# Attention of the first halves: weights from query-by-key scores, turned through VectorE and DRAM

## The chip, the core and the metric

The kernel runs on one core of a Trainium2 chip. The core has a matrix engine (TensorE, PE in the profile; its weight loads are listed as PEld), VectorE (DVE), ScalarE (ACT), GpSimd (POOL) and SyncE (SP), which here only issues transfers. Each engine runs its own queue of instructions in the order in which they were written; an instruction whose inputs are not there yet stops everything behind it on that engine. Data lie in SBUF (128 partitions), matrix results in PSUM, and DRAM is reached by DMA.

The metric is the device time of one execution in microseconds, as the median of several. For the kernel before it is 3506.4 us, from three runs between 3506.35 and 3508.18.

## The reference

One transformer block with modulation by a condition, in float32: 8 sequences of 1024 rows of 512, 16 heads of 32 columns, an MLP of 2048.

```
mod = silu(condition) @ Wada + bada          # shifts, scales and gates, per sequence
xm  = layernorm(x, g1, be1) * (1 + sc_a) + sh_a
q, k, v = split(xm @ Wqkv)                   # 16 heads
scores  = q @ k.T * 32 ** -0.5, causal mask
x = x + gt_a * ((softmax(scores) @ v) @ Wproj + bproj)
xm = layernorm(x, g2, be2) * (1 + sc_m) + sh_m
x = x + gt_m * (gelu(xm @ W1 + b1) @ W2 + b2)
```

The part in question is the softmax and the product with v. In a matrix product on TensorE the summed index lies on the partitions. Scores with queries on the partitions (query by key) give maxima and sums along a row easily, but the product with v needs the weights with keys on the partitions.

## The kernel before

**Blocks.** The 16 half sequences of 512 rows are blocks n = 0 to 15. An even block is the first half of its sequence and attends to its own 512 keys; an odd block attends to its own keys and those of the block before. Heads go in four groups g of four; the four heads of a group sit on 32 partitions each, and their matmuls run side by side.

**Attention.** Because the mask is causal, the 512 x 512 triangle of a group is cut into tiles of 128 rows and 512, 384, 256 or 128 columns, which are packed into *units* of 512 columns by four heads: the widest alone, 384 with 128, and 256 with the 256 of the next group. That makes 2.5 units a group and 10 a block; an odd block has 16 whole units more. Each unit is computed twice:

- A *score unit* (`scores_at_once`, L1588) computes query-by-key scores into the PSUM tile `st`/`sc` (L1595), adds the mask (L1607) and takes row maxima (L1610) on VectorE. `split_maxima` splits the maxima into three bfloat16 parts, and `maxima_rows` turns them into a row per group with small matmuls (L1648).
- A *weight unit* (`weights_T`, L1663) computes the scores once more, now key by query: it starts each PSUM tile with minus the maxima (L1674) and adds the products (L1686). ScalarE takes the exponential (L1698) into a buffer `pT`, POOL zeroes the masked corner (L1703). `weigh` (L1715) multiplies with v (L1726), `add_weights` (L1801) adds the units of a group on POOL (L1816), and `finish` (L1736) sums over keys with a matmul against ones (L1747), inverts on VectorE (L1765) and multiplies on POOL (L1790).

There is a single score tile of four PSUM banks, used by both kinds of units in turn, and three buffers `pT` (`free_p`), handed out when written and given back when read.

**The linear work.** All other products are written as a sequence of steps per window w (`plan`): projections k, q and v, the output projection `proj`, the MLP (`u`, `d`) and the LayerNorm tiles (`at`, `mt`). The large products use Strassen's scheme with seven products of half size; nearly all of them are `matmul` (L217). `at` and `mt` turn normalized rows: VectorE transposes squares of 32 x 32 (L700), the tile is written to DRAM (`held`, L709) and read back with rows and squares exchanged (L714). Weights come through a ring of eight buffers of 256 KB (`fetch`): a load is issued when PE has used the buffer eight pieces before.

**What sets the order.** The program is laid out by a planner at build time. Every helper notes an assumed duration on its engine (`note`, `note_pe`, `note_act`, `note_dma`) and when its result will be there (`written`) or its buffer free (`left`). Linear steps are generators that yield what they wait for. `attend` goes through the blocks; before each unit, `step_aside` lets linear work go ahead until the unit's inputs are due by these assumed times, and a rate (`stream`) spreads the linear work of a window over its units. `until` runs linear work until a condition holds. So each engine's order is fixed before the kernel runs, by assumed times; on the chip an instruction that is reached early simply waits. All weight loads, LayerNorm tiles and results share SyncE's one queue, in the same fixed order.

Of the kernel before, what the change touches and what calls it, by code (L numbers as in the profile page):

```python
# [22 lines left out]
def kernel(  # L23
# [33 lines left out]
    nc = tc.nc  # L57
# [196 lines left out]
    for w in range(1, NB):  # L254
# [182 lines left out]

    cond_act = tmp.tile([P, TB], F32, tag="top", name="cond_act", bufs=1)[:B, :]
    nc.scalar.activation(cond_act, cond_sb, AF.Silu)
# [113 lines left out]
    def add_job(job, reads, first=False):  # L553

        at = sum(1 for other in jobs if other[2]) if first else len(jobs)
        jobs.insert(at, (job, reads, first))

    def run_jobs(everything=False):
        while jobs and (
            everything or (now["DVE"] <= now["PE"] and due(jobs[0][1]) <= now["PE"])  # L560
        ):
            jobs.pop(0)[0]()
# [33 lines left out]
    def hurry():  # L596

        while jobs and due(jobs[0][1]) <= now["PE"] + 500:
# [881 lines left out]
    TRIANGLE = [[0], [1, 3], [2]]  # L1480
    groups = [(n, g) for n in range(NB) for g in range(NC)]

# [175 lines left out]

    free_p = list(range(3))
    first_end, unadded = (0, NC - 1), []  # L1660
    outs, totals = {}, {}

    def weights_T(n, g, parts):  # L1663
# [18 lines left out]
        for k, c0, w, gg in parts:  # L1682
# [11 lines left out]
            note_pe(2.5 * COLUMN * w, "rows", reads, ["st"])  # L1694
        slot = free_p.pop(0)
        pT = pp.tile([P, HPG, TB], F32, tag=f"p{slot}", name=f"pT_{n}_{g}_{parts[0][0]}")
# [39 lines left out]
    def finish(n, g):  # L1736
# [7 lines left out]
        for i, (c0, w, term, held) in enumerate(terms):  # L1744
# [6 lines left out]
            note_pe(2 * COLUMN * w, "columns", [("acc", n, g), ("p", held)], [("l", bank)])  # L1751
        free_p.extend([slot, *(held for *_, held in more)])
# [23 lines left out]
        if (n, g) == first_end:  # L1776
# [5 lines left out]
            return  # L1782

        def quotient():
            invert(3)
            if n == NB - 1 and g == NC - 2:
# [32 lines left out]
    def attend():  # L1819
        previous = None  # L1820
        for n in range(NB):
            h = blocks[n][1]
            slots = []
            mine = sum(exp_need(parts) for g in range(NC) for parts in weight_units(n, g))
            for g in range(NC):
# [4 lines left out]
                for k in range(n_slots):  # L1830
                    upto = len(units)
                    if nxt < len(groups):
# [4 lines left out]
                        if k == n_slots - 1 and nxt + 1 < len(groups):  # L1837
# [36 lines left out]
    def close(n, g, parts, pT, slot, last):  # L1874

        until(lambda: n - blocks[n][1] + parts[-1][0] // NTT in valued)
        own, other = [[part for part in parts if (part[3] == g) == of] for of in (True, False)]
        weigh(n, g, own, pT, slot, last)
        if other:
            shared[n, g + 1] = other, pT, slot  # L1880
        elif parts[0][0] > 0 and (n, g) != first_end:
            free_p.append(slot)
        if parts[0][0] == 0:
            totals[n, g] = (pT, slot)
            if (n, g) in shared:
# [3 lines left out]
                if (n, g) != first_end:  # L1889
                    free_p.append(slot)  # L1890
        if last:
            finish(n, g)

    def next_scores():
# [15 lines left out]

    needs = sum(exp_need(parts) for n in range(NB) for g in range(NC) for parts in weight_units(n, g))
    needs += sum(score_need(*unit) for unit in units)
    for n in range(NB):
# [80 lines left out]
```

## Time and profile before

| what | value |
|---|---|
| median of three runs | 3506.4 us (3506.35 to 3508.18) |
| the profiled execution | 3510.74 us, with a span of 3509.0 us from the first to the last instruction |
| granted TensorE clock | 0.998 |
| busy share of the span | PE 98%, PEld 49%, DVE 63%, ACT 35%, POOL 59% |
| DMA | 491 MB, queue on SyncE 47.1% of 16 engines' span |

The page of the profile has the busy time of each engine, the chain of work that ended last (followed back from the last instruction to what released it), the costliest groups of instructions with the mean of one and the idle time ahead of them, and the DMA queues. The trace gives more: what waited for what, the instructions in order of time, and tables by stretch. A line number names the line of the kernel that issued an instruction. Records of matmuls overlap, so that the cost on PE is better read from start to start. Matmuls in float32 have two records each.

### The profile page before, as it was taken

The numbers are of one execution on the slowest core, as the hardware profiler recorded it, in microseconds if no ns is written. First come the engines' busy times: TensorE is split into PE (matmuls) and PEld (weight loads), VectorE is DVE, ScalarE is ACT, GpSimd is POOL, SyncE is SP. The second block draws the span as 40 slices with busy tenths as digits, with TensorE's granted clock in tenths as the row PEclk, the third lists the DMA queues.
The fourth block names the chain that finished last, engine by engine and source line by source line (L and its number), as shares of the span: only waits on it lengthen the run. The fifth ranks groups of instructions, "written<-read, shape, count | busy, mean of one in ns | idle before, by whom it ended". The sixth has DMA issues, their size and how long they took to land.

```text
span 3509.0 us, 120365 instructions
## 1 busy us (share of the span) xinstructions
PE 3454.3 (98%) x54429; PEld 1724.0 (49%) x54429; DVE 2198.9 (63%) x2401; ACT 1212.4 (35%) x1276; POOL 2084.2 (59%) x2258
## 2 busy tenths in 40 slices
PE   8999999999999999999999999999999999999999
PEld 4444445445554545445454454544555444554445
DVE  5766676564666656665666566765666756656563
ACT  2335333342233423335223342333423343232531
POOL 3767846666366663756727576275753658537660
PEclk9999999999999999999999999999999999999999
DMA  6843444535545445363454534545354544443334
GB/s 212 263 137 104 137 115 140 142 107 159 142 125 156 119 147 153 119 170 115 137 157 130 155 117 144 150 137 148 116 155 137 165 122 146 128 136 101 96 121 140
DMA packets 328194, 491.10 MB, mean 140 GB/s; under 512 B 27260, under 2 KB 177596, under 8 KB 324100
## 3 DMA queue, kind: packets, MB, share of 16 engines
q1 hardware_dynamic: 327568, 483.39, 47.1%
q8 instruction: 428, 7.01, 0.8%
q14 instruction: 82, 0.67, 0.1%
q10 hardware_dynamic: 116, 0.03, 0.0%
HBM read 425.57 MB, written 55.64 MB: 137 GB/s over the span
## 4 chain that ended last, share of the span: by engine, by line
PE 83%; POOL 7%; DMA 3%; DVE 3%; ACT 1%; issue 1%; SPq 1%; ACTq 0%; DVEq 0%; POOLq 0%
PE bank L217 59%; PE sc L1595 8%; PE st L1686 6%; PE po L1726 6%; POOL pT L1816 4%; PE st L1674 2%; PE bank L1747 2%; DMA hat_m<-held_m 1%; DVE mx L1610 1%; POOL hT L170 1%; ACT pT L1698 1%; DMA held_m<-xm_m 1%; PE bank L1648 0%; POOL xr L170 0%; DMA w<-in_L_cond_Wqkv_dram 0%
## 5 line engine op out<-in xcount | busy, mean ns | idle before, releaser
L1816 POOL TENSOR_TENSOR pT<-pT,pT 128x256 f32<-128x256 f32 (+3 forms) x1254 | 1219.7, 1007 | 298.5 <-PE po L1726 181.6
L1698 ACT ACTIVATE pT<-st 128x2048 f32<-128x2048 f32 x288 | 540.9, 1878 | 1065.1 <-PE st L1686 959.8
L217 PE MATMUL bank<-w,hT 128*32 128x256 f32 x14336 | 823.7, 380 | 0.4 <-issue 0.4
L1610 DVE TENSOR_REDUCE mx<-sc 128x4 f32<-128x2048 f32 (+3 forms) x384 | 665.9, 1755 | 235.6 <-PE sc L1595 229.5
L217 PEld LDWEIGHTS bank<-w,hT 128*32 128x32 f32 x14336 | 446.7, 110 | 390.3 <-issue 105.8
L217 PE MATMUL bank<-xm_m,w 128*32 128x256 f32 x8192 | 498.6, 381 | 3.6 <-ACT xm_m L774 2.2
L217 PE MATMUL bank<-t_m,w 128*32 128x256 f32 x6144 | 382.4, 380 | 0.9 <-DVE t_m L786 0.6
L217 PEld LDWEIGHTS bank<-xm_m,w 128*32 128x32 f32 x8192 | 255.6, 110 | 231.2 <-issue 62.2
L1703 POOL TENSOR_SCALAR_AFFINE_SELECT pT<-pT 128x512 f32<-128x512 f32 x256 | 167.5, 672 | 331.9 <-ACT pT L1698 329.4
L1607 DVE TENSOR_TENSOR sc<-sc,mask 128x1024 f32<-128x1024 f32 (+1 forms) x160 | 162.8, 1018 | 293.3 <-PE sc L1595 237.8
L1595 PE MATMUL sc<-kT,qT 32*128 32x512 f32 (+3 forms) x3072 | 329.5, 521 | 4.3 <-ACT pT L1698 3.3
L1726 PE MATMUL po<-pT,v 128*32 128x512 f32 (+3 forms) x3048 | 301.6, 490 | 3.9 <-POOL pT L1703 3.9
L1686 PE MATMUL st<-qT,kT 32*128 32x512 f32 (+3 forms) x3072 | 300.8, 487 | 0.0
L217 PEld LDWEIGHTS bank<-t_m,w 128*32 128x32 f32 x6144 | 189.6, 110 | 172.9 <-issue 48.5
L1765 DVE RECIPROCAL rec<-rec 128x128 f32<-128x128 f32 x256 | 227.3, 922 | 48.2 <-ACT rec L1756 48.2
L217 PE MATMUL bank<-xm_a,w 128*32 128x256 f32 x3968 | 243.4, 382 | 0.4 <-DMA w<-in_L_cond_Wqkv_dram 0.4
L217 PE MATMUL bank<-w,qT 128*32 128x512 f32 x2048 | 237.0, 595 | 1.1 <-DMA w<-in_L_cond_Wproj_dram 0.7
L1595 PEld LDWEIGHTS sc<-kT,qT 32*128 32x128 f32 x3072 | 129.6, 183 | 188.2 <-issue 88.4
L208 DVE TENSOR_TENSOR hT<-bank,u_u 128x512 f32<-128x512 f32 x187 | 126.6, 686 | 105.8 <-PE bank L217 103.1
L217 PE MATMUL bank<-t_a,w 128*32 128x256 f32 x2944 | 183.2, 380 | 0.0
L217 PEld LDWEIGHTS bank<-xm_a,w 128*32 128x32 f32 x3968 | 123.5, 110 | 110.3 <-issue 29.3
L1115 ACT ACTIVATE hT<-hT,cols 128x512 f32<-128x512 f32 x256 | 164.7, 712 | 35.9 <-DVE hT L208 28.5
(243 smaller groups left out, 3404.0 us busy)
## 6 DMA issues: line engine op xcount, KB each, us to landing
w<-in_L_cond_W_dram SPq DMA_DIRECT2D x384, 256.0 KB
w<-kept_up_S SPq DMA_DIRECT2D x256, 256.0 KB
w<-kept_down_S SPq DMA_DIRECT2D x256, 256.0 KB
w<-kept_qkv_S SPq DMA_DIRECT2D x180, 256.0 KB
w<-in_L_cond_Wqkv_dram SPq DMA_DIRECT2D x147, 256.0 KB
hat_a<-in_x_dram SPq DMA_DIRECT2D x64, 256.0 KB
xr<-in_x_dram SPq DMA_DIRECT2D x32, 512.0 KB
w<-in_L_cond_Wproj_dram SPq DMA_DIRECT2D x64, 256.0 KB
```

The lines of the kernel that those rows point to most:

```text
L208: nc.vector.tensor_tensor(out, src, other, op)
L217: nc.tensor.matmul(ps[r, :], columns, rhs, start=start, stop=stop, skip_group_check=True)
L1115: nc.scalar.activation(hT[:, i, :], hT[:, i, :], AF.Gelu, bias=cols[:, O_B1 + f : O_B1 + f + 1])
L1595: nc.tensor.matmul(sc[:, j, c0 : c0 + w], qTs[n][r, gg, ts(qt, P)], keys_of(n, kh)[r, gg, :w], start=True, stop=True, skip_group_check=True,)
L1607: nc.vector.tensor_tensor(place, place, shape_of.to_broadcast(place.shape), ALU.add)
L1610: nc.vector.tensor_reduce(maxima[n, gg][:, kh, qt, :], sc[:, :, c0 : c0 + w], axis=AX.X, op=ALU.max)
L1686: nc.tensor.matmul(st[:, j, c0 : c0 + w], kT[r, gg, ts(k % NTT, P)], qT[r, gg, TB - w :], start=False, stop=True, skip_group_check=True,)
L1698: nc.scalar.activation(pT[:, :, :used], st[:, :, :used], AF.Exp, scale=scale)
L1703: nc.gpsimd.affine_select(diagonal, diagonal, pattern=[[0, HPG], [1, P]], compare_op=ALU.is_ge, fill=0.0, base=0, channel_multiplier=-1,)
L1726: nc.tensor.matmul(po[r, TB - w :], v[:, k % NTT, g * P + j * hd : g * P + (j + 1) * hd], pT[:, j, c0 : c0 + w], start=(k == 0), stop=last ...
L1765: nc.vector.reciprocal(some, some)
L1816: nc.gpsimd.tensor_tensor(into, into, pT[:, j, c0 : c0 + w], ALU.add)
```

## The change

Blocks 2, 4, ..., 14 (all even blocks but the first) compute each unit once. `attend_rows` goes through a block's ten units with `rows_unit`, and `gather` finishes a group:

1. The scores are computed query by key into the score tile, masked, and reduced to row maxima on VectorE as before; the maxima times minus the scale become a bias.
2. ScalarE takes the exponential at once, one head and one tile at a time, with the bias and with the row sums as a second output. It writes into one of the three buffers, with the columns put in an order that suits step 4.
3. VectorE inverts the sums; POOL or ScalarE, whichever the planner sees free earlier, multiplies the weights by them.
4. VectorE transposes the buffer of 128 x 2048 in squares of 32 x 32, in place.
5. Four or eight DMAs, of 32 partitions each, write the squares to a tile in DRAM (`image`) at their place. The buffer is then given back.
6. When all of a group is there, `gather` reads it back as three *pages* with keys on the partitions: two of 1 MB into buffers of the same three, one of 0.5 MB into the tile that `finish` uses for its copies (`top` and `rec` are now two halves of it). Each page is multiplied with v as it lands, in pieces of 256 and 128 columns, and the finished sum is copied into place. There is nothing left to divide.

For these blocks the second score pass, the minus maxima, the split and the rows of maxima, the corner masks, the additions on POOL, the sums over ones and the division fall away. Only one unit at a time may be between step 2 and step 5. The scores of the odd block after a rows block start beside its last units. The odd block's products with v wait until all groups before it are gathered. Blocks 0, 1 and all odd blocks compute as before. In windows of even blocks from 4 on, the projection of v moves behind the output projection and the LayerNorm tile of the block before; the rate of all windows from 2 on is multiplied by 0.95.

```diff
             steps = late + [("v", w)] + rows_a + [("proj", n), ("mt", n), ("k", w + 1)]
+            if w > 3 and not blocks[w][1]:
+                steps = late + rows_a + [("proj", n), ("mt", n), ("v", w), ("k", w + 1)]
...
-    groups = [(n, g) for n in range(NB) for g in range(NC)]
+    def by_rows(n):
+        return n > 1 and blocks[n][1] == 0
+    groups = [(n, g) for n in range(NB) for g in range(NC) if not by_rows(n)]
...
-        top = tmp.tile([P, TB], F32, tag="top", name=f"top_{n}_{g}", bufs=1)
-        rec = tmp.tile([P, TB], F32, tag="rec", name=f"rec_{n}_{g}", bufs=1)
+        both = tmp.tile([P, 2, TB], F32, tag="top", name=f"top_rec_{n}_{g}", bufs=1)
+        top, rec = both[:, 0, :], both[:, 1, :]
...
+            if by_rows(n):
+                attend_rows(n, previous)
+                previous = None
+                continue
...
-            stream["rate"] = planned_time(n) / mine * (0.7 if n == 0 else 1.0)
+            stream["rate"] = planned_time(n) / mine * (0.7 if n == 0 else 0.95 if n > 1 else 1.0)
...
+        if blocks[n][1] and by_rows(n - 1):
+            until(lambda: (n - 1, NC - 1) in gathered)
...
+    def rows_unit(n, g, parts):
+        until(lambda: n in projected)
+        until(lambda: free_p and len(raws) < 1)
+        slot = take_slot()
...
+                nc.tensor.matmul(
+                    sc[:, j, c0 : c0 + w], qTs[n][r, gg, ts(qt, P)], kTs[n][r, gg, :w],
+                    start=True, stop=True, skip_group_check=True,
+                )
...
+        nc.vector.tensor_tensor(place, place, shape_of.to_broadcast(place.shape), ALU.add)
...
+            nc.vector.tensor_reduce(mx[:, i, :], sc[:, :, c0 : c0 + w], axis=AX.X, op=ALU.max)
...
+        nc.vector.tensor_scalar(minus[:, :n_parts], mx[:, :n_parts], -scale, None, ALU.mult)
...
+                nc.scalar.activation(
+                    tile_of[:, j], sc[:, j, c0 : c0 + w].rearrange("p (k b x) -> p k b x", b=NTT, x=hd),
+                    AF.Exp, bias=minus[:, i, j : j + 1], scale=scale, accum_out=total[:, i, j : j + 1],
+                )
...
+            nc.vector.reciprocal(total[:, :n_parts], total[:, :n_parts])
...
+                nc.gpsimd.tensor_tensor(tile_of, tile_of, by, ALU.mult)
...
+                    nc.scalar.activation(tile_of[:, j], tile_of[:, j], AF.Copy, scale=total[:, i, j : j + 1])
...
+            nc.vector.transpose(raw, raw)
...
+                for a in range(NTT):
+                    into = images[n, gg][qt // 2][:, qt % 2, a, :count, :]
+                    nc.sync.dma_start(
+                        into.rearrange("(b k) s e -> k b (s e)", k=hd),
+                        raw[ts(a, hd), at : at + HPG * w].rearrange("k (b f) -> k b f", b=NTT),
+                    )
...
+    def gather(n, g):
...
+            for into, source, ns in moves:
+                nc.sync.dma_start(into, source)
+                note_dma(ns, [], [key])
+            for rows_of, at, k, qt in sets:
+                yield [key, ("v", n), ("v done", n)], ["po"] if out is None else []
...
+                    nc.tensor.matmul(
+                        out[r, qt * P : qt * P + wide],
+                        vs[n][:, k, g * P + j * hd : g * P + (j + 1) * hd],
+                        page[:, rows_of, at, r],
+                        start=start_, stop=i == 2, skip_group_check=True,
+                    )
```

More of the change, by code (lines that the diff above doesn't have):

```diff
@@ L556, in add_job, with run_row_jobs @@
         jobs.insert(at, (job, reads, first))
+    row_jobs = []
+    def run_row_jobs(everything=False):
+        while row_jobs and (everything or now["DVE"] <= now["PE"]):
+            first = min(row_jobs, key=lambda job: due(job[1]))
+            if not everything and due(first[1]) > now["PE"]:
+                return
+            row_jobs.remove(first)
+            first[0]()
     def run_jobs(everything=False):
+        run_row_jobs(everything)
         while jobs and (
@@ L596, in hurry @@
     def hurry():
+        while row_jobs and min(due(job[1]) for job in row_jobs) <= now["PE"] + 500:
+            run_row_jobs(True)
         while jobs and due(jobs[0][1]) <= now["PE"] + 500:
@@ L1659, with count_slots, take_slot, give_slot @@
     free_p = list(range(3))
+    SLOT, BESIDE = "a page", "a page for rows"
+    def count_slots():
+        written[SLOT] = 0.0 if free_p else NEVER
+    def take_slot():
+        slot = free_p.pop(0)
+        count_slots()
+        return slot
+    def give_slot(slot):
+        free_p.append(slot)
+        count_slots()
     first_end, unadded = (0, NC - 1), []
@@ L1782, in finish @@
             return
+        written["top used"] = NEVER
         def quotient():
+            written["top used"] = 0.0
             invert(3)
@@ L1889, in close, with row_units, row_need @@
                 if (n, g) != first_end:
-                    free_p.append(slot)
+                    give_slot(slot)
         if last:
             finish(n, g)
+    images, raws, gathered, in_image = {}, [], set(), {}
+    written["pages"] = 0.0
+    def row_units(n):
+        todo = []
+        for g in range(NC):
+            mine = [parts for _, _, parts in score_units(n, g)]
+            todo += [(g, parts) for parts in mine[2:] + mine[:2]]
+        return todo
+    def row_need(n, g, parts):
+        return score_need(n, g, parts) + 400 + 1900 * sum(part[3] for part in parts) / TB
@@ new lines, in attend_rows @@
+    def attend_rows(n, previous):
+        todo = row_units(n)
+        lo = unit_at[0]
+        more = len(score_units(n + 1, 0)) + 1
+        ends = [lo] * (len(todo) - 3) + [lo + (i + 1) * more // 4 for i in range(3 - 1)] + [lo + more]
+        mine = sum(row_need(n, *unit) for unit in todo)
+        mine += sum(score_need(*unit) for unit in units[lo : ends[-1]])
+        stream["rate"] = planned_time(n) / mine
+        written["free for k", n + 1] = 0.0
+        for g in range(NC):
+            written["image", n, g] = NEVER
+            written["spread", n, g] = NEVER
+            in_image[n, g] = 0
+        for (g, parts), upto in zip(todo, ends):
+            rows_unit(n, g, parts)
+            run_excursions(1)
+            pace(row_need(n, g, parts))
+            if previous is not None:
+                close(*previous)
+                previous = None
+                for i in (n, n + 1):
+                    written["free for v", i] = 0.0
+            while unit_at[0] < upto:
+                ns = score_need(*units[unit_at[0]])
+                next_scores()
+                run_excursions(1)
+                pace(ns)
```

136 lines of the change are left out of this document (128 added, 8 removed).

## The prediction

> **What bounds the kernel now.** First the page: shares of the engines, then the chain that ended last.
>
> ```profile
> span 3509.0 us, 120365 instructions
> PE 3454.3 (98%) x54429; PEld 1724.0 (49%) x54429; DVE 2198.9 (63%) x2401; ACT 1212.4 (35%) x1276; POOL 2084.2 (59%) x2258
> PE 83%; POOL 7%; DMA 3%; DVE 3%; ACT 1%; issue 1%; SPq 1%; ACTq 0%; DVEq 0%; POOLq 0%
> PE bank L217 59%; PE sc L1595 8%; PE st L1686 6%; PE po L1726 6%; POOL pT L1816 4%; PE st L1674 2%; PE bank L1747 2%; DMA hat_m<-held_m 1%; DVE mx L1610 1%; POOL hT L170 1%; ACT pT L1698 1%; DMA held_m<-xm_m 1%; PE bank L1648 0%; POOL xr L170 0%; DMA w<-in_L_cond_Wqkv_dram 0%
> ```
>
> TensorE (PE) is idle for 55 us of 3509, and its own work is 83% of the chain. So work taken from PE counts in full, and anything added elsewhere counts only where PE comes to wait for it. Next, PE's waits, and what the DMA queue on SyncE waits for.
>
> ```profile
> PE st L1674 <- DVE mx L1610: 7.8, 8, 2.4
> PE sc L1595 <- ACT pT L1698: 3.3, 6, 0.8
> PE sc L1595 <- DVE mx L1610: 0.5, 1, 0.5
> SPq L360 <- PE bank L217: 1412.0, 639, 18.9
> ```
>
> The three waits on the score tile (L1674, L1595) sum to 11.6 us, and SyncE mostly waits for PE to free a weight buffer: loads are ahead of need.
>
> **What PE loses.** The timeline shows pieces of one block; start to start is what PE really pays, since records overlap.
>
> ```profile
> 1006.68 1.04 PE L1747 MATMUL bank<-pT,ones 128*32 128x512 f32 x8
> 1007.65 0.40 PE L1674 MATMUL st<-mrow,minus_ones 32*128 32x512 bf16 x4
> 1007.88 1.03 PE L1686 MATMUL st<-qT,kT 32*128 32x512 f32 x8
> 1008.84 2.80 PE L217 MATMUL bank<-w,hT 128*32 128x256 f32 x48
> 1008.98 1.88 ACT L1698 ACTIVATE pT<-st 128x2048 f32<-128x2048 f32 x1
> ...
> 1016.76 1.14 PE L1595 MATMUL sc<-kT,qT 32*128 32x512 f32 x8
> 1017.83 4.09 PE L217 MATMUL bank<-w,hT 128*32 128x256 f32 x72
> 1017.97 2.29 DVE L1610 TENSOR_REDUCE mx<-sc 128x4 f32<-128x2048 f32 x1 [6.03 <-PE sc L1595]
> ...
> 1913.54 0.41 PE L1648 MATMUL bank<-ident_b,mcols 128*32 128x128 bf16 x16 [0.84 <-POOL mcols L1632]
> 1913.78 1.03 PE L1726 MATMUL po<-pT,v 128*32 128x512 f32 x8
> ```
>
> A group of four heads in an even block has 2.5 units of 512 columns. The second score pass costs 1008.84 - 1007.65 = 1.19 us a unit, 2.98 a group; the sums over ones 1007.65 - 1006.68 = 0.97; the row of maxima 0.24. That is 4.19 us a group, and 7 blocks x 4 groups give **-117 us**. The first score pass (1.07 us) stays. The weighted sums of v stay too, but in pieces of 256 and 128 columns.
>
> ```profile
> L1726 PE MATMUL po<-pT,v 128*32 128x512 f32 x1528 | 200.9, 597 | 3.2 <-POOL pT L1703 3.2
> L1726 PE MATMUL po<-pT,v 128*32 128x256 f32 x512 | 39.7, 382 | 0.0
> L1726 PE MATMUL po<-pT,v 128*32 128x128 f32 x504 | 25.3, 273 | 0.2 <-POOL pT L1703 0.2
> ```
>
> Eight records are one piece of four heads: 1.05, 0.63 and 0.40 us, with the tail of each. By these, pieces of 256 instead of 512 cost up to 0.2 us more each, some 10 us in all; back to back the tails overlap, so I take **+3** (0 to 10).
>
> **What the other engines get.**
>
> ```profile
> 1937.27 2.48 DVE L700 STREAM_TRANSPOSE xm_m<-hat_m 128x512 f32<-128x512 f32 x4
> L1765 DVE RECIPROCAL rec<-rec 128x128 f32<-128x128 f32 x256 | 227.3, 922 | 48.2 <-ACT rec L1756 48.2
> L1759 ACT COPY top<-po 128x512 f32<-128x512 f32 x64 | 37.9, 593 | 0.0
> L774 ACT ACTIVATE xm_a<-hat_a,shifta,gaina 128x512 f32<-128x512 f32 x44 | 32.5, 805 | 22.7 <-DMA hat_a<-held_a 15.2 <-DMA w<-kept_qkv_S 7.5
> L1816 POOL TENSOR_TENSOR pT<-pT,pT 128x512 f32<-128x512 f32 x504 | 662.0, 1346 | 209.5 <-ACT pT L1698 114.5 <-PE po L1726 92.7
> L1703 POOL TENSOR_SCALAR_AFFINE_SELECT pT<-pT 128x512 f32<-128x512 f32 x256 | 167.5, 672 | 331.9 <-ACT pT L1698 329.4
> ```
>
> - VectorE: 70 transposes of 2048 columns, 2.48 us each by the four in the first row, +174; 112 reciprocals of 0.92 gone, -103; some 40 evacuations move to it. About 2300 us, two thirds of the span.
> - ScalarE: 70 exponentials of 1.88 (131 us) become 448 of one head and 128 to 512 columns. No row shows an accumulating exponential; a 512-wide copy is 0.59 and a scaled one 0.81, so an estimate of 196 to 260 us. In the instruction order 47 of the 70 units are normalized here (288 instructions of at most 0.81). With 84 fewer copies: about 1400 us, 40%.
> - POOL: 336 additions of 384, 256 and 128 columns go (by the 512-wide row an estimate of 226 us), with 112 masks of 0.67 (75 us); 23 normalizations of up to 4 x 1.35 (124 us) come: down some 180 us.
>
> The step that projects v of an even block moves behind the output projection before it; in the instruction order it still ends over 150 us of PE work before the first page is used, so it costs nothing. No total gets near the span, so I cost their totals at nothing; the cover is PE's linear work. What isn't covered is latency: where PE, in order, reaches an instruction too early.
>
> **Wait 1: the pages back from DRAM.** Each unit goes out in 4 or 8 DMAs of 32 partitions (448 in all); each group comes back in three pages, two of 1 MB and one of 0.5 MB (140 DMAs, 84 pages). 588 issues of about 0.44 us and 147 MB join SyncE's one queue. The nearest rows are the LayerNorm tiles, which go out and come back the same way: stretches of traffic, then issues and the consumer.
>
> ```profile
> 1768.50:1772.50 4.00, 4.00 (x88) 2.40 (x84) 2.87 (x4) 2.72 (x3) 1.22 (x2) 1.00 0.96 336
> 1775.50:1781.50 6.00, 6.00 (x120) 3.56 (x116) 2.08 (x3) 1.07 (x1) 6.00 (x10) 1.00 0.94 208
> ```
>
> ```profile
> q1 hardware_dynamic: 327568, 483.39, 47.1%
> ```
>
> ```profile
> 1768.46 0.34 SPq L709 DMA_DIRECT2D held_m<-xm_m  x1
> 1774.50 1.75 SPq L714 DMA_DIRECT2D hat_m<-held_m  x4
> 1783.10 2.22 ACT L774 ACTIVATE xm_m<-hat_m,shiftm,gainm 128x512 f32<-128x512 f32 x3 [6.53 <-DMA hat_m<-held_m]
> ```
>
> In the first fence the last columns are DMA share and GB/s. 1 MB over all partitions ran at 336 GB/s and was usable 6.0 us after its issue, with other traffic beside it; 1 MB in four DMAs of 32 partitions ran at 208 GB/s and took 8.6 us. A page is one to three DMAs over all partitions in runs of 0.5 to 1 KB, so it lies between: alone 2.9 us of latency plus 3.1 of transfer is 6.0, and the base load (the queue holds the DMA engines for 47% of the span) adds about 1. I take 7.0 us for 1 MB, 5.3 for half of it; ends 5.2 and 8.6.
>
> Against this stands PE's work between issue and use. In the changed kernel's instruction order I priced PE's instructions with the rows above, times 1.04 (3509 over the 3378 that this pricing gives for the kernel before), and put each page's issue behind the last weight buffer that SyncE waits for. Mean cover is 7.8 us for the big pages and 6.0 for the small; in blocks 6 to 12 the last page has 0.9. Summed over 84 pages, PE waits 14 us if a big page takes 5.2, 40 at 7.0, 90 at 8.0, 126 at 8.6. I take **+40**.
>
> **The clock behind a long wait.** The last page of blocks 6, 8, 10 and 12 holds PE for 5.3 - 0.9 = 4.4 us. The trace has one such gap near its end:
>
> ```profile
> PE bank L764 <- ACT hat_m L687: 3.5, 3, 2.7
> ```
>
> ```profile
> 3400.00:3410.00 10.00, 6.53 (x51) 4.41 (x55) 5.46 (x12) 4.53 (x7) 1.07 (x1) 0.66 0.27 90
> 3410.00:3420.00 10.00, 10.00 (x192) 5.52 (x184) 2.77 (x4) 1.65 (x3) 5.65 (x5) 1.00 0.46 136
> ```
>
> PE was busy for 6.53 of 10 us, the granted clock was 0.66, and 1.00 in the next 10. At worst 3.4 us are lost beside the idle time, at best none, as part of the slow clock fell into it. I take half, 1.7 for each of 4 gaps: **+7**. [...] By the row's upper end the sum would be 14, and the total 3474.
>
> **Wait 2: the score tile.** One PSUM tile serves every score pass. A first pass holds it from 1016.76 until the reduction ends at 1017.97 + 2.29, 3.5 us; a second pass until 1008.98 + 1.88, 3.2. Even blocks now hold it once, for pass, mask, reduction and exponentials, where they held it twice: 1.2 + 1.2 + 2.3 + some 3 us with the mask row below.
>
> ```profile
> L1607 DVE TENSOR_TENSOR sc<-sc,mask 128x1024 f32<-128x1024 f32 x96 | 118.2, 1232 | 170.1 <-PE sc L1595 126.6 <-issue 21.6 <-ACT top L1759 13.4
> ```
>
>  The order packs odd blocks tighter: uses with under 0.5 us to spare go from 144 to 236, and the sum by which PE comes too early from 13 to 26 us. So +13, and 0.08 us (11.6 / 144) for 92 more tight uses, +7: **+20**, from -8 (the waits shown, gone) to 45.
>
> **Wait 3: SyncE behind a scatter or a page.** A weight load behind one has 10.7 us of PE work before its use in all but a few per cent of cases, the same as before. I take **+8**, 0 to 30 (1 us at each of 28 first pages).
>
> **Sum.** -117 + 3 + 40 + 7 + 20 + 8 = -39. From the profiled execution's 3510.7 that is 3471.7; it stands 4.3 above the median of 3506.4, so the median comes to **3467**.
>
> **The rivals.**
> [...]
> 2. *Slower: late pages.* 8.6 us as in the row of 208 GB/s, with 147 MB more on the queue: -117 + 3 + 126 + 14 + 20 + 8 = +54, 3560. It decides from about 8.0 us a page on. Against: pages use all partitions.
> 3. *Slower: the score tile.* Each of the 236 tight uses waits 0.4 us, 94 instead of 20: +35, 3541. The exponentials' unknown price and VectorE's transposes speak for it.
> 4. *Nothing comes of it.* An even block has to end with its last page before its output projection can start; if that chain, not PE's work, sets a block's length, 16.7 us a block turn into waiting: 3506.
>
> **Chances.** Forecast 0.42, clean 0.23, late pages 0.20, score tile 0.08, nothing 0.07. A measurement tells 0.2% (7 us) from no change. Nothing splits into 0.05 same, 0.01 faster and 0.01 slower: faster 0.66, same 0.05, slower 0.29. The likeliest alone ranges from 3440 to 3495; 8 in 10 is 3410 to 3535, which cuts off some of rival 1 and the upper half of 2 and 3.
>
> **What would show it.** Right: second-pass, ones and maxima records fall (the exponentials of second passes from 288 to 218), PE busy is near 3350, and PE's waits on the page tiles sum to about 40 us, the longest about 4 us, four times. Wrong: page waits near 100 us, or waits of the score passes on ScalarE or VectorE far above 30, a granted clock under 0.99, or weight loads that PE waits for.

## The result, and the profile after

The changed kernel takes 3658.8 us (median of 4 runs, 3657.4 to 3663.6), against 3506.4 for the kernel before on the same chip: a ratio of 1.0436, with an interval of 1.0418 to 1.0454. The forecast was 3467, with 3535 as its upper end; the time lies above even the rival with late pages (3560). All the PE work that was to go did go, and more came back than it was worth.

The page of the changed kernel (shares of the engines, then the queue on SyncE):

```profile
span 3655.7 us, 118781 instructions
PE 3409.0 (93%) x52861; PEld 1701.2 (47%) x52861; DVE 2307.2 (63%) x2563; ACT 1379.6 (38%) x2246; POOL 1830.1 (50%) x1754
q1 hardware_dynamic: 494672, 630.23, 58.0%
```

Two things are seen here. PE's idle time, span less busy, was 54.7 us and is 246.7: +192. And PE's busy time fell by only 45 us (3454.3 to 3409.0), though about 114 us of matmuls went: the remaining ones ran more slowly. The mean granted clock is 0.975; it was 0.998. Summing busy time times (1 - granted clock) over windows of 1 us gives 72.4 us of PE time lost to a slow clock, against 5.4 before. Busy time less this loss is the work itself: 3336.6 against 3448.9, so 112 us less. Between runs with the same matmuls this difference varies by some 10 us (3440.8 to 3449.1 in the runs without rows below), so it is no finer than that.

What PE waits for (total, times, longest):

```profile
PE po L2122 <- DMA turned<-image: 134.1, 57, 7.2
PE sc L1615 <- ACT rows_p L2021: 16.7, 13, 6.3
PE bank L217 <- DVE p_v L194: 13.4, 10, 3.8
PE po L1761 <- POOL pT L1738: 9.5, 9, 2.8
PE st L1708 <- DVE mx L1630: 7.2, 5, 3.2
PE sc L1615 <- ACT pT L1733: 5.1, 7, 1.1
PE po L1761 <- ACT qT L2140: 4.2, 6, 0.7
```

The pages alone are 134 us, and nothing like that row stood in the profile before. The rest of PE's idle time is 246.7 - 134.1 = 112.6 us, 58 more than the 54.7 before. So the whole difference of the two spans is

| term | us |
|---|---|
| work taken from PE | -112 |
| PE waits for pages | +134 |
| PE's other waits | +58 |
| slower clock while PE works (72.4 - 5.4) | +67 |
| sum; the spans differ by 3655.7 - 3509.0 = | +147 |

The slow clock follows the waits. A stretch of the timeline, then the same microseconds in windows (after the time come busy us and records of PE, its weight loads, VectorE, ScalarE and POOL; then granted clock, DMA share and GB/s):

```profile
1810.55 1.48 SPq L2112 DMA_DIRECT2D turned<-image  x3
1815.30 1.94 PE L2122 MATMUL po<-turned,v 128*32 128x256 f32 x24 [3.06 <-DMA turned<-image]
```

```profile
1812.00:1813.00 1.00, 0.24 (x8) 0.00 (x0) 1.00 (x3) 1.00 (x3) 0.00 (x0) 1.00 0.86 254
1813.00:1814.00 1.00, 0.00 (x0) 0.00 (x0) 0.51 (x1) 1.00 (x4) 0.00 (x0) 1.00 1.11 365
1814.00:1815.00 1.00, 0.00 (x0) 0.00 (x0) 0.00 (x0) 0.48 (x2) 0.00 (x0) 0.84 1.01 279
1815.00:1816.00 1.00, 0.70 (x8) 0.46 (x12) 0.00 (x0) 0.00 (x0) 0.00 (x0) 0.50 1.11 281
1816.00:1817.00 1.00, 1.00 (x21) 0.87 (x17) 0.00 (x0) 0.00 (x0) 0.00 (x0) 0.50 1.03 391
1817.00:1818.00 1.00, 1.00 (x19) 0.60 (x12) 0.00 (x0) 0.00 (x0) 0.00 (x0) 0.50 1.06 364
1818.00:1819.00 1.00, 1.00 (x24) 0.60 (x20) 0.35 (x1) 0.00 (x0) 0.00 (x0) 0.95 1.15 312
```

PE waits 3.06 us for a page and then works 2.7 us at half speed: 1.4 us more on top of the wait. The DMA share is at 1 or above from 1813 on: by this measure the engines that bring the page have no idle time.

### The profile page after: what moved, and what is told of

Its sections match the earlier page's. It is cut to its first block, busy times and chain, and to the rows that moved or that the text cites. A ratio compares the mean times of both kernels' runs of the same rounds, so it can differ in the third digit from the quotient of the medians.

```text
span 3655.7 us, 118781 instructions
## 1 busy us (share of the span) xinstructions
PE 3409.0 (93%) x52861; PEld 1701.2 (47%) x52861; DVE 2307.2 (63%) x2563; ACT 1379.6 (38%) x2246; POOL 1830.1 (50%) x1754
## 5 line engine op out<-in xcount | busy, mean ns | idle before, releaser
L1855 POOL TENSOR_TENSOR pT<-pT,pT 128x512 f32<-128x512 f32 (+3 forms) x918 | 973.4, 1094 | 309.7 <-ACT pT L1733 157.1
L1733 ACT ACTIVATE pT<-st 128x2048 f32<-128x2048 f32 x218 | 409.4, 1878 | 650.8 <-PE st L1720 462.1
L1630 DVE TENSOR_REDUCE mx<-sc 128x4 f32<-128x2048 f32 (+3 forms) x272 | 502.8, 1865 | 215.0 <-PE sc L1615 211.8
L2021 ACT ACTIVATE rows_p<-rows_sc,rows_minus 128x256 f32<-128x256 f32 (+3 forms) x448 | 229.3, 534 | 445.6 <-DVE rows_minus L2015 284.4
L2040 POOL TENSOR_TENSOR rows_p<-rows_p,rows_sum 128x1024 f32<-128x1024 f32 (+3 forms) x40 | 85.3, 2149 | 401.1 <-DVE rows_sum L2030 210.5
L1615 PE MATMUL sc<-kT,qT 32*128 32x512 f32 (+3 forms) x2176 | 257.2, 561 | 23.9 <-ACT rows_p L2021 16.7
L1761 PE MATMUL po<-pT,v 128*32 128x512 f32 (+3 forms) x2176 | 238.9, 530 | 13.9 <-POOL pT L1738 9.5
L1720 PE MATMUL st<-qT,kT 32*128 32x512 f32 (+3 forms) x2176 | 228.0, 510 | 0.0
L2122 PE MATMUL po<-turned,v 128*32 128x256 f32 (+1 forms) x1344 | 87.5, 378 | 134.1 <-DMA turned<-image 134.1
L1627 DVE TENSOR_TENSOR sc<-sc,mask 128x1024 f32<-128x1024 f32 (+1 forms) x90 | 91.6, 1017 | 149.5 <-PE sc L1615 125.3
```

What stands on the lines that cost most here:

```text
L1615: nc.tensor.matmul(sc[:, j, c0 : c0 + w], qTs[n][r, gg, ts(qt, P)], keys_of(n, kh)[r, gg, :w], start=True, stop=True, skip_group_check=True,)
L1627: nc.vector.tensor_tensor(place, place, shape_of.to_broadcast(place.shape), ALU.add)
L1630: nc.vector.tensor_reduce(maxima[n, gg][:, kh, qt, :], sc[:, :, c0 : c0 + w], axis=AX.X, op=ALU.max)
L1720: nc.tensor.matmul(st[:, j, c0 : c0 + w], kT[r, gg, ts(k % NTT, P)], qT[r, gg, TB - w :], start=False, stop=True, skip_group_check=True,)
L1733: nc.scalar.activation(pT[:, :, :used], st[:, :, :used], AF.Exp, scale=scale)
L1761: nc.tensor.matmul(po[r, TB - w :], v[:, k % NTT, g * P + j * hd : g * P + (j + 1) * hd], pT[:, j, c0 : c0 + w], start=(k == 0), stop=last ...
```

## The experiments

For each run the profiled execution gives PE's idle time (span less busy), its waits on pages, and the PE time lost to a slow clock (summed as above). The ratio is to the kernel before on the same chip; the runs were on four chips, on which its medians were 3506.3 to 3510.4. The profiled execution is one of several and not always near the median: it was the fastest for `fill_zero` (3634.0), `old_plan` (3637.6), `no_scatter` (3542.3) and `no_traffic_old` (3499.1), and the slowest for `page_late4` (3611.0), `together_late4` (3620.0) and `no_traffic2` (3523.9).

| run | median us | ratio (95%) | PE idle | page waits | slow clock |
|---|---|---|---|---|---|
| before | 3506.4 | 1 | 54.7 | 0 | 5.4 |
| changed kernel | 3658.8 | 1.0436 (1.0418 to 1.0454) | 246.7 | 134.1 | 72.4 |
| `tile_only` | 3510.1 | 1.0001 (0.9992 to 1.0011) | 53.8 | 0 | 6.0 |
| `plan_rate1` | 3527.3 | 1.0061 (1.0046 to 1.0076) | 71.1 | 0 | 10.2 |
| `plan_v_early` | 3531.1 | 1.0064 (1.0049 to 1.0079) | 74.1 | 0 | 14.1 |
| `plan_only` | 3536.1 | 1.0075 (1.006 to 1.009) | 81.4 | 0 | 9.0 |
| `one_block` | 3552.5 | 1.0132 (1.0116 to 1.0147) | 101.7 | 13.4 | 21.5 |
| `fill_zero` | 3645.5 | 1.0382 (1.0358 to 1.0406) | 145.1 | 36.6 | 27.0 |
| `page_late4` | 3604.4 | 1.0271 (1.0256 to 1.0286) | 219.9 | 64.8 | 57.9 |
| `together` | 3604.7 | 1.0272 (1.0251 to 1.0293) | 206.2 | 83.6 | 61.2 |
| `together_late4` | 3613.8 | 1.0301 (1.0284 to 1.0318) | 222.1 | 40.5 | 60.1 |
| `old_plan` | 3649.6 | 1.0409 (1.0381 to 1.0436) | 236.4 | 113.9 | 62.9 |
| `together_old` | 3654.4 | 1.0423 (1.0405 to 1.0442) | 253.3 | 88.0 | 56.9 |
| `no_scatter` | 3557.5 | 1.0139 (1.0122 to 1.0156) | 165.6 | 58.0 | 36.6 |
| `page_part2` | 3535.7 | 1.0089 (1.0073 to 1.0106) | 157.9 | 34.8 | 41.8 |
| `no_traffic2` | 3515.7 | 1.0015 (0.9999 to 1.003) | 148.3 | 31.5 | 44.3 |
| `no_traffic_old` | 3506.2 | 0.9994 (0.9984 to 1.0004) | 136.5 | 23.2 | 29.1 |

**The planning edits without rows.** `plan_only` takes the changed kernel and lets no block go by rows.

```diff
     def by_rows(n):
-        return n > 1 and blocks[n][1] == 0
+        return False
```

> The changed kernel with no block computed by rows: what is left is the place of the projection of v, the rate of 0.95 and the joined tile for top and rec. Theory (pages that land late, and the clock behind each wait): these edits cost nothing, 3495 to 3520 us, clock 0.998. Rival (the new order of the linear work costs it): 3550 us or more, with waits of PE in even blocks.

It measured 3536.1, 26 us above the 3510.4 of the kernel before on the same chip: between the two expectations, more than a free edit, and a sixth of the loss. PE's work is unchanged (busy 3452.3). Three edits remain in it, and three later runs took them apart: the planner's rate back to 1.0 (`plan_rate1`), the projection of v back in its place (`plan_v_early`), both (`tile_only`).

```diff
-            if w > 3 and not blocks[w][1]:
-                steps = late + rows_a + [("proj", n), ("mt", n), ("v", w), ("k", w + 1)]
...
-            stream["rate"] = planned_time(n) / mine * (0.7 if n == 0 else 0.95 if n > 1 else 1.0)
+            stream["rate"] = planned_time(n) / mine * (0.7 if n == 0 else 1.0)
```

> No rows, and the planner's rate back from 0.95 to 1.0; of the planning edits only the later projection of v (and the shared tile) remains. If the rate is what cost 26 us: 3506 to 3515. If the moved projection is: 3528 to 3540. If half and half: near 3520.

> No rows, planner's rate 1.0 and v projected where it was: of the whole change only the shared tile of quotient and reciprocal and its slot bookkeeping remain. If the shared tile costs nothing, 3506 to 3512, and the 19 us of the run before are the moved projection. If the shared tile, which the reciprocal cannot enter until the quotient has left it, makes PE wait: 3520 to 3530.

> No rows, planner's rate 0.95, v projected where it was. If rate and moved projection cost 9 and 19 us and add: 3515. If the shared tile is what costs: 3525 to 3540.

The shared tile of quotient and reciprocal costs nothing (3510 against 3508). The moved projection alone costs some 19 us (3527.3 less 3508.7), the rate alone some 23 (3531.1 less 3508.0), both together 26: they do not add. The run with the rate alone lands in the range that was expected if the shared tile cost time, but `tile_only` rules the tile out. The waits of PE in the run with the moved projection, and then in the one with the rate:

```profile
PE bank L217 <- POOL qT L1829: 16.6, 4, 12.0
```

```profile
PE bank L217 <- ACT hT L1129: 15.6, 3, 5.2
PE st L1706 <- DVE mx L1628: 12.5, 17, 2.4
```

Moving v brings the output projection forward, and once it then stands 12 us before the last quotient of POOL that it reads. The other rate gives other long waits in other places.

**One row block.** `one_block` computes block 8 alone by rows.

```diff
     def by_rows(n):
-        return n > 1 and blocks[n][1] == 0
+        return n == 8
```

> Rows in block 8 alone; blocks 2, 4, 6, 10, 12, 14 as before; the planning edits stay. If each row block costs the same, it stands one seventh of 3659 - 3536 = 123 us above the planning edits alone: 3536 + 18 = 3554. If a row block costs only through its neighbours (the next one's traffic, the slots it leaves), it shows PE's saved work, 16 us: about 3520.

3552.5: the planning edits plus 16.4 us, and seven times 16.4 is 115 of the 123 us between `plan_only` and the changed kernel. (The two ran on different chips; by the differences to the kernel before on each, one block adds 20 us, and seven 143 of 127.) So a row block loses by itself, not through its neighbours. It takes 16 us of work from PE and adds 13.4 of waits on pages, 7 of other idle time (101.7 - 13.4 - 81.4) and 12.5 of slow clock (21.5 - 9.0).

**The clock by itself.** `fill_zero` lets PE multiply zeros into the same output ahead of the pages that it waited for; the numbers of groups follow the waits in the trace of the changed kernel, 287 groups in all. The zeros add nothing to that output.

```diff
+    FILL = {(0, 1): 6, (1, 0): 7, (1, 2): 2, (2, 0): 2, (2, 2): 5, (3, 0): 5, (3, 1): 3, (3, 2): 11}
...
+                for some in range(FILL.get((g, i), 0) if rows_of is sets[0][0] and sets[0][1:] == (at, k, qt) else 0):
+                    for j in range(HPG):
+                        r = slice(j * hd, (j + 1) * hd)
+                        nc.tensor.matmul(
+                            out[r, qt * P : qt * P + wide],
+                            zeros,
+                            vs[n][:, k, :wide],
+                            start=start_ and some == 0,
+                            stop=False,
+                            skip_group_check=True,
+                        )
+                start_ = start_ and not FILL.get((g, i), 0)
```

> Ahead of the pages that PE waits for (eight of twelve in a block), PE multiplies v with zeros into the same sums, 0.44 us a group, for about as long as the wait was (41 groups a block, 126 us in all); the order is the same. Theory of the clock (each gap of about 3 us is followed by 3.4 us at half clock, some 80 us in all): granted clock 0.99 or more, PE's waits on pages under 50 us, and the time falls by 40 to 80 us to 3580 to 3620, although PE has 126 us more to do. Rival (the waits alone are the loss): the time stays or rises, 3650 to 3700 us.

```profile
PE po L2138 <- DMA turned<-image: 36.6, 34, 2.7
```

```profile
1813.00:1814.00 1.00, 0.54 (x12) 0.26 (x12) 1.00 (x2) 0.00 (x0) 0.00 (x0) 1.00 1.02 403
1814.00:1815.00 1.00, 1.00 (x28) 0.57 (x24) 0.59 (x2) 0.59 (x1) 0.00 (x0) 1.00 1.10 461
1815.00:1816.00 1.00, 1.00 (x20) 0.58 (x16) 0.34 (x1) 0.00 (x0) 0.00 (x0) 1.00 0.88 357
```

The clock stays at 1.00 (0.991 over the run), and the loss to it falls from 72.4 to 27.0. The time falls by only 13 us (23 between the profiled executions): PE's busy time is 78.2 higher, its idle time 101.6 lower. Where the clock no longer falls, 45 us are won; the zeros, placed by a fixed table, overshoot the waits and take about half of it back. So the clock term is real; the time lies between the two expectations, since the zeros cost PE more than the idle time that they fill.

**Pages later in the plan.** In `page_late4` the planner believes that a page lands 4 us later than it did, and so puts more other work of PE ahead of it.

```diff
                 nc.sync.dma_start(into, source)
                 note_dma(ns, [], [key])
+            written[key] += 4000
```

> The planner takes each page to land 4 us later than it did; nothing else is changed. Theory (a page lands about 4 us after the time that the order was made for): PE's waits on pages fall from 134 us to under 50, the clock rises from 0.975 to 0.985 or more, and the time falls to 3540 to 3610 us. Rival (the block's chain of units and pages sets its length, and there is no other work to put in between): the waits move to the steps behind the last page, and the time stays above 3640 us.

```profile
PE po L2123 <- DMA turned<-image: 64.8, 20, 15.1
PE bank L217 <- DVE p_v L194: 32.8, 10, 5.2
PE sc L1615 <- ACT rows_p L2021: 20.8, 17, 3.9
PE st L1708 <- DVE mx L1630: 15.6, 13, 3.2
```

Page waits fall by 69 us; 54 come off the time, which is in the theory's range. Its mechanism holds in part only: page waits were to be under 50 us and the clock 0.985, and they are 64.8 and 0.977. Other waits rise by some 42 us: the work pulled forward is reached before its own inputs (`p_v`, which is the projection of v, from 13.4 to 32.8). And the clock recovers little (57.9 us lost); the waits that are left are fewer and longer (20, up to 15.1 us). In this order there was not enough other work of PE that was ready; that no order could find it is not shown.

**Pages requested together.** `together` requests the second and third page of a group with the first, where their buffers are free; `together_late4` adds the 4 us.

```diff
+            for later in range(i + 1, 3):
+                if later not in got and ready(later):
+                    load(later)
```

> The three pages of a group are requested together wherever their buffers are free, instead of each when PE is about to need it; nothing else changes. Theory A (a page is asked for too late: PE reaches it 6.5 to 8 us after the request, and each wait of 3 us also costs slow clock): the waits on second and third pages, about 117 of the 134 us, fall by half where a buffer is free, and the clock rises to about 0.985; 3590 to 3630 us. Rival B (the DMA engines are full in these stretches, so pages requested together only share the same bytes a second): waits move from the later pages to the first, 3640 to 3670.

> As before, and the planner takes a page to land 4 us later than it did, so that it puts other work of PE ahead of the first use. Theory A: what the later estimate alone gave (3604) and part of the earlier requests on top, 3560 to 3600. Rival B (DMA engines full): no better than the later estimate alone, 3600 to 3640.

Requesting earlier takes 50 us of page waits and 54 us of time, as much as the later estimate; both together give nothing more. The gain is on the later pages: waits on second and third pages fall from 74 to 22 us (they were 74 of the 134, not 117 as the expectation has it), and those on first pages stay at 60. So the pages requested together did not merely push the waits to the first.

**The planning edits undone under the rows.** `old_plan` keeps all row blocks and undoes the rate and the moved v; `together_old` also requests pages together.

> All row blocks stay; the two planning edits are undone (the planner's rate back from 0.95 to 1.0, the projection of v back ahead of the normalization). If these edits cost the row blocks what they cost without rows (26 us), 3633; if row blocks need them, 3660 or more; if they cost nothing here because PE waits anyway, 3650 to 3665.

> Pages of a group requested together, and both planning edits undone. If the two gains add (54 and 9): 3596. If undoing the edits only paid because PE waited on pages: 3605 or more. Neither comes near 3506.

The first is 9 us below the changed kernel, with intervals that overlap. In its waits the projection of v is gone (13.4 to 2.8), and another stands in its place:

```profile
PE po L2120 <- DMA turned<-image: 113.9, 56, 5.1
PE bank L217 <- DVE xm_m L782: 24.2, 5, 7.9
```

In the second that same wait is 47.6 us. Page waits fall (88.0), but the time is 3654.4: the gain of the earlier requests is lost to other waits. What the orders gain one at a time does not add.

**Less traffic.** `no_scatter` leaves out the writes of the squares from block 4 on; the pages read block 2's.

```diff
+                if n > 2:
+                    images[n, gg] = kept_images[gg]
...
                 for a in range(NTT):
                     into = images[n, gg][qt // 2][:, qt % 2, a, :count, :]
-                    nc.sync.dma_start(
...
+                    if n == 2:
+                        nc.sync.dma_start(
```

> Blocks 4 to 14 don't write their squares to DRAM; their pages are read from what block 2 wrote (so weights of another block). Order and planner are the same; 63 MB fewer are moved. Theory A (the DMA engines are full while a block goes through its units, so pages queue): PE's waits on pages fall from 134 to 40 to 80 us, and the time to 3540 to 3600 us. Theory B (pages are issued too late, and their own transfer is what PE waits for): waits stay above 100 us, and the time above 3630 us.

```profile
PE po L2126 <- DMA turned<-image: 58.0, 42, 6.3
```

PE's order is the same, yet page waits fall from 134.1 to 58.0 us and the time by 101 us. When a page was there is seen only where PE waited for it. From block 4 on, such a first page of a group was there 7.5 us after its request in the median (9 cases), against 8.2 (21 cases) in the changed kernel; a last page 5.7 (13) against 6.7 (17). So the writes delay a page by some 0.7 to 1.0 us. The run does not separate their load on the DMA engines from their place on the queue: in the changed kernel 12 page requests also waited for writes to land, and that row is gone here too.

```profile
SPq L2112 <- DMA image<-rows_p: 16.3, 12, 2.5
```

`page_part2` keeps the writes and reads one square in eight (or four) of each page; PE's matmuls are as many and as wide, with that square in place of the others.

```diff
+                if n > 2:
+                    into, source = into[:, :1], source[:, :1]
                 nc.sync.dma_start(into, source)
...
-                        page[:, rows_of, at, r],
+                        page[:, rows_of, at, r] if n == 2 else page[:, rows_of.start : rows_of.start + 1, at, r].to_broadcast([P, wide // hd, hd]),
```

> From block 4 on, only one of the eight (or four) squares of each page's run is read back, and PE takes that square again for the others: the same matmuls, one eighth of the reads, all writes kept; the output is not the reference's. Theory (what a page costs is its way through full DMA engines): a page lands in about 5 us, PE's waits on pages fall from 134 to 15 to 35 us and about 50 us of slow clock go with them: 3470 to 3510. Rival (the writes of the squares ahead of it on the queue set the landing, the page's own size does not): landing stays near 7 us, 3560 to 3610.

```profile
PE po L2124 <- DMA turned<-image: 34.8, 19, 4.8
PE sc L1615 <- ACT rows_p L2021: 17.7, 16, 6.3
```

From block 4 on, a last page that PE waited for is now there after 3.8 us (8 cases), and page waits are where the theory had them, at the upper end. The time, 3535.7, is above its range: the clock gave back 31 us instead of 50 and the other waits rose by 10.

`no_traffic2` joins the two: all work of the engines stays, and the way through DRAM is all but gone from block 4 on.

> The same, and the squares of blocks 4 to 14 are not written either: PE's, VectorE's, ScalarE's and POOL's work are those of the changed kernel, the way through DRAM is all but gone; the output is not the reference's. Theory (the way through DRAM and the clock behind its waits are the loss): 3659 - 120 - 60 = 3479 less some of the other waits, 3440 to 3480, so faster than before. Rival (the row blocks' own order, with the score tile held through mask, reduction and exponentials and squares turned on VectorE, costs PE what it saves): 3506 or more.

```profile
PE po L2128 <- DMA turned<-image: 31.5, 12, 4.2
PE sc L1615 <- ACT rows_p L2022: 18.4, 17, 6.6
PE bank L217 <- DVE hT L1228: 13.0, 3, 4.3
PE bank L217 <- DVE p_v L194: 11.1, 11, 1.2
PE st L1708 <- DVE mx L1630: 9.4, 7, 3.2
PE po L1761 <- POOL pT L1738: 6.8, 5, 2.8
```

143 of the 152 us go with the way through DRAM. (Without the writes alone it was 101, without most of the reads alone 123: the two do not add.) But the theory's 3440 to 3480 is missed: at 3515.7 the change, freed of most of what it was losing by, is still no faster than the kernel before. PE's work is 119 us less here (3373.7 - 44.3 against 3448.9), and against it stand 31.5 us of page waits (14.7 of them in block 2, which keeps its traffic), 62 of other waits (148.3 - 31.5 - 54.7) and 39 of clock: +13, as the spans have it (3522.0 - 3509.0).

`no_traffic_old` asks whether the planning edits make those other waits; it undoes them there.

> The row blocks nearly without their way through DRAM, and with both planning edits undone; the output is not the reference's. Theory (without the way through DRAM PE's saved 114 us were eaten by other waits, 62 us, and the clock behind them, 39; the planning edits cause some 26 of these waits): 3516 - 26 and some of the clock, 3470 to 3490. Rival (the other waits come from the row blocks' own chain, whatever the planner does): 3505 to 3525.

```profile
PE po L2126 <- DMA turned<-image: 23.2, 14, 5.9
PE bank L217 <- DVE xm_m L782: 17.8, 5, 6.9
PE st L1706 <- DVE mx L1628: 11.2, 7, 3.2
PE sc L1613 <- ACT rows_p L2020: 4.8, 13, 0.5
```

3506.2, no difference from before, as the rival had it. The planning edits are some 9 us here by the medians, with intervals that overlap; the score tile's wait on the exponentials shrinks and another wait grows. Freed PE time turns into idle time and slow clock under either order. Which link of the row blocks' chain does it stays open, and whether a better order would keep the gain was not tried. None of the versions is faster than the kernel before.

## Why the prediction was wrong

- **What PE loses: right.** -114 forecast, -112 measured, closer than the measure itself is good for. Second-pass exponentials fell from 288 to 218:

```profile
L1733 ACT ACTIVATE pT<-st 128x2048 f32<-128x2048 f32 x218 | 409.4, 1878 | 650.8 <-PE st L1720 462.1 <-POOL pT L1855 111.0 <-POOL mcols L1651 32.1
```

- **What the other engines get: right for VectorE and ScalarE.** VectorE 2307 us (2300 forecast), ScalarE 1380 (1400). POOL fell by 254 us instead of 180, as its additions saved 248 instead of 226 and its normalizations took 85 instead of 124. Each of ScalarE's new exponentials has a second record that reads the sum out, about 0.2 us, most of it beside the next: from start to start 512 columns cost 0.68 us, the 448 of all sizes some 230, within the estimate of 196 to 260.

```profile
1891.51 0.69 ACT L2021 ACTIVATE rows_p<-rows_sc,rows_minus 128x512 f32<-128x512 f32 x1
1892.10 0.19 ACT L2021 ACTIVATION_READ_ACCUMULATOR rows_p<-rows_sc,rows_minus 128x1 f32 x1
1892.19 0.68 ACT L2021 ACTIVATE rows_p<-rows_sc,rows_minus 128x512 f32<-128x512 f32 x1
```

- **Wait 1, the pages: the first failed step.** I took 7.0 us for a big page and 5.3 for a small one, 40 us in all, and measured 134. The step failed in both of its parts, the landing and the cover. A first page took 8.2 us in the median and a last one 6.7, where PE waited. Without the writes it was 7.5 and 5.7; what I left too small was the price of what runs beside a page, of which that run shows the writes; that of the weight loads no run shows. I took the load of the whole span, 47%, where the row phase runs near 1 (first line; the second is a stretch without pages):

```profile
1800.00:1850.00 50.00, 42.80 (x716) 24.95 (x712) 32.14 (x42) 19.04 (x55) 2.14 (x3) 0.93 0.97 289
2000.00:2050.00 50.00, 50.00 (x735) 22.58 (x728) 38.71 (x42) 18.48 (x18) 36.61 (x43) 1.00 0.53 159
```

  The prediction's own table had 90 us at 8.0, so a landing some 1 us later is about half of the miss. The rest is cover: from its request until PE came to need it, a big page had 7.1 us on average and a small one 5.1, where I had 7.8 and 6.0. With the cover of each page as it was, even 7.0 and 5.3 would have made some 90 us, an estimate from the requests and first uses in the trace. The four long waits of last pages in blocks 6 to 12 were there, 4.5 to 7.2 us for the forecast 4.4; the many shorter ones were not foreseen. SyncE's queue shows one case of a late request: the page is issued behind the writes of the unit before, some LayerNorm tiles and a weight load.

```profile
1824.47 4.19 SPq L2065 DMA_DIRECT2D image<-rows_p  x5
1828.71 1.89 SPq L730 DMA_DIRECT2D hat_m<-held_m  x4
1830.70 0.39 SPq L360 DMA_DIRECT2D w<-in_L_cond_Wqkv_dram  x1
1831.13 0.52 SPq L2112 DMA_DIRECT2D turned<-image  x1
```

- **The clock: the second failed step.** Four gaps at 1.7 us, +7, against +67. The price was about right: the granted clock left 1.00 in 36 places, in 3 before, at 2.0 us each (67 / 33). The count was wrong. That four waits of 4.4 us alone would cost clock was my estimate, and no run shows it. In the trace of the changed kernel a clock of 0.50 followed, within 3 us of their end, 7 of 11 PE waits of 2.25 to 2.75 us that began at full clock, 11 of 14 of 2.75 to 3.25, all 15 longer ones, and 6 of 33 between 1 and 2.25. I had a row that pointed there, a clock of 0.66 behind waits of at most 2.7 us, and counted the longer waits alone.
- **Wait 2, the score tile: right in size.** The score tile's waits rose from 11.6 us to some 30 (16.7 + 7.2 + 5.1 and small ones), so +18 for +20 forecast.
- **Steps costed at nothing.** The later projection of v was to cost nothing, as it ends long before the first page is used. That looked at who waits for it, not at what moves forward in its place: without rows it costs 19 us. The planner's rate of 0.95 I gave no price at all; without rows it is 23. Under the rows their share is not separable (9 us, with intervals that overlap). PE's other waits are +58 us, where the sum had 28: the score tile has 18 of them and the projection of v (`p_v`, 13.4) the next largest share; the rest is spread over many rows, and which of them the planning edits cause is not shown.
- **Wait 3, weight loads behind pages: right in that they cost little.** No such wait stands among the larger ones.
- **The rivals.** Late pages (3560) had the right mechanism and too small a clock term: with the measured 134 + 67 for its 126 + 14, and 58 for the other waits, it gives +145 and 3651. That its 126 comes near 134 is partly luck: its 8.6 us was above the measured 8.2, and its cover was too long as well. "Nothing comes of it" had a point that I gave 7 in 100: without the way through DRAM the change is at 3506 to 3516, and PE's freed time turns into waiting. So the premise that work taken from PE counts in full did not hold either: in `no_traffic2` 119 us of work went, and the time did not fall.

The sum of my terms, with the measured ones: -112 + 134 + 67 + 58 = +147 instead of -117 + 3 + 40 + 7 + 28 = -39.

## What to carry to other kernels

Price a transfer by the load of the stage in which it runs, not by the span's mean (here a DMA share of 0.97 among the pages, for 47% before), and count what the change itself puts on the queue ahead of it. On an engine that is 98% busy, removed work is worth its time only if the next instruction's inputs come earlier by as much (in `no_traffic2` 119 us of work went, and no time); price the chain that feeds it before counting the gain. The many waits here, 57 on pages with 134 us in all, came with 67 us of slow clock, so one should price their number, not only their length.

## What the runs showed of the hardware

- In the trace of the changed kernel the granted clock fell to 0.50 behind PE waits, not always: 7 of 11 of 2.25 to 2.75 us that began at full clock, all 15 above 3.25 us, at some 2.0 us of lost PE time for each slow stretch. All 36 slow stretches of this trace begin on one grid of 3.413 us, and all but the last, which the end of the run cuts off, are one to four steps of it long. Of its 1011 steps at full clock, PE was idle for more than 0.6 of the time (2.05 us) in 32, and half clock followed all of them; 0.5 to 0.6 in 14, and it followed 4; less in 965, and it followed none. The four waits of 2.36 to 2.57 us that no slow stretch followed were all split between two steps, with at most 2.00 us in one.
- In the changed kernel an exponential with row sums on ScalarE is two records (448 of each), the second of which reads the accumulator; the pair takes 0.68 us from start to start for 512 columns.
- In `fill_zero` zero matmuls held the clock up through the waits (0.991 over the run, for 0.975), and 45 us less were lost to it; the time fell by 13 us only, as 124 us of zeros replaced 102 us of idle time.
